# A Flamingo block on one core: TensorE's order at the start of a q unit, and new places for the next block's preparation

## The chip, the cores and the metric

The kernel runs on one NeuronCore of a Trainium2 chip. The metric is the time of one execution on the device, in microseconds (us); the median of several runs is compared. All arithmetic is in 32-bit floating point. A NeuronCore has five engines with queues of their own: TensorE (PE in the profile, with its weight loads listed apart as PEld), VectorE (DVE), ScalarE (ACT), GpSimd (POOL) and SyncE (SP), which here only issues transfers.

## The reference

Eight sequences of 512 tokens with 512 features go through four residual steps, each behind a layer norm: linear attention over 64 context tokens, a feed-forward network of width 2048, a softmax cross attention, and a feed-forward network of eight expert groups with a router. The change lies in the first of them, the linear attention:

```python
x = x + jnp.tanh(g_xattn[0]) * _L0_xattn_ref(_layernorm(x), ctx_2048, Wq, Wg, bg, Wkv, Wo)

# _L0_xattn_ref(query, kv, ...), 16 heads of 32 features
q = query @ Wq.T
gate = sigmoid(query @ Wg.T + bg)
k, v = split(kv @ Wkv.T)
q, k = feature_map(q), feature_map(k)        # x + 1 if x > 0 else exp(x)
kv_summary = einsum('bhsd,bhse->bhde', k, v)
k_sum = k.sum(axis=-2)
z = 1 / (einsum('bhld,bhd->bhl', q, k_sum) + eps)
attn = einsum('bhld,bhde->bhle', q, kv_summary) * z
out = (attn * gate) @ Wo.T
```

## The kernel before, in words

**Blocks and units.** Context keys and values are summed up for all sequences at the start (to about 46 us). Then a loop over eight blocks b, one for each sequence, does the linear attention; after it come eight blocks of each feed-forward network. An attention block has three units: q (`QUp`), gate (`GUp`) and down (`ODown`). Every unit is a product of two matrices that are cut in two by two, done with seven half-sized products instead of eight (the scheme of Strassen and Winograd). Products have the numbers 1 to 7, and a unit runs them in the order 1, 2, 6, 5, 7, 4, 3. I write q1, g4, o7 and so on. Each product is four matmuls of 128x128 by 256 columns, which the profile shows as eight TensorE instructions.

**Banks.** Products 1, 6, 7 and 4 accumulate one onto the other in one PSUM bank (`x`), 5 and 3 in another (`w`), and 2 alone in a third (`z`). Between two products of one bank, ScalarE or VectorE must read the sum so far: in q and gate units ScalarE copies it (line 925), in the down unit VectorE adds it into the residual x (line 1045). There are four banks in rotation for all three units.

**Steps.** `steps` deals out the first five products of a unit, and holds 4 and 3 back as late: they follow the first product of the next unit. So a q unit has seven steps n: q1 (n = 0), then the late o4 and o3 of the down unit before it (n = 1, 2), then q2, q6, q5, q7 (n = 3 to 6). In block 0 there is nothing late, so the steps are q1, q2, q6, q5, q7; in block 1, which has no down unit before it, the late products are g4 and g3 of block 0. Between the q unit and the gate unit stand the numerators (pn) of the block before, and beside the gate unit the denominators (pd). One down unit belongs to the block before: it runs behind the gate unit.

**Order.** A scheduler lays the instructions of each engine in an order of its own, by its own estimates of when each is ready. An engine named in the set `in_order` is exempt: each instruction written while it is in the set is queued behind the one that was written last for that engine. In the attention loop only GpSimd and SyncE are in the set throughout; `with here("vector")` and the like put others in for a few lines. An instruction written outside such lines may still be moved ahead of earlier ones.

**Preparation.** While block b runs, a generator `prep` (`prep_xa0`, which calls `normed`) prepares the input of block b + 1, a piece at each call of `some(prep)`. For blocks 2 to 7 the pieces are:
1. mean and variance of the four token tiles on VectorE (pinned, by `here("vector")`), then 1 / sqrt and shift on GpSimd;
2. normalisation of tiles 0 and 1 on ScalarE, transpose of tile 0 on VectorE (all pinned);
3. normalisation of tiles 2 and 3, transposes of tiles 1 and 2;
4. transpose of tile 3;
5. sixteen transfers issued by SyncE, which bring the pieces to their places in `xnT`, the operand of the next block's products;
6. the generator's last mark, without an instruction.
The rest of the generator (`token_combinations`, the sums `S` of the operand's quarters, lines 689 to 692) is run at step 4 of the down unit. The normalised tiles lie in the same buffer as `spread`, the denominators of the block before; the buffer comes free when `gated` (line 1288) has used these.

**Other work in the loop.** `tick` lets `build_first` prepare the weights of the feed-forward network: transfers, and combinations on VectorE (the tiles `raw_up` and `build_ff_down`), pinned in VectorE's order. `gated` and `attended` (lines 1288 and 1316) join denominators, gate and numerators on VectorE, `features` (lines 675 to 677) is the feature map of q.

Of the kernel before, what the change touches and what calls it, by code (L numbers as in the profile page):

```python
# [31 lines left out]
B, S, D = 8, 512, 512  # L32
# [36 lines left out]
def flamingo_kernel(  # L69
# [26 lines left out]
    @contextmanager  # L96
    def here(*engines):

        new = {*engines} - in_order
        in_order.update(new)  # L100
        yield
        in_order.difference_update(new)
# [59 lines left out]
    def load_x(ph, b):  # L162
        if ph == "xa0" and b % 4 == 3:
            t = awork.tile([P, NT, D], F32, tag="x4", name=f"x_{ph}{b}")
        else:
            t = work.tile([P, NT, D], F32, tag="x", name=f"x_{ph}{b}", bufs=3)
        if ph == "xa0":
            src = x[ts(b, S), :].rearrange("(t p) d -> p t d", p=P)
        else:
            src = between[ph, b]  # L170

        queue = nc.scalar if ph == "xa0" and b > 1 else nc.sync
        with here("scalar"):
            queue.dma_start(out=t, in_=src)
        xs[ph, b] = t
# [3 lines left out]
    def flush():  # L179
        while stores:  # L180
            store_x(*stores.pop(0))
# [767 lines left out]
    def combine_inner(at, prefix=""):  # L949

        a11, a12, a21, a22, s1, s2 = (inner[prefix + k][:, at, :] for k in INNER)
        nc.vector.tensor_tensor(s1, a21, a22, ALU.add)
        nc.vector.tensor_tensor(s2, s1, a11, ALU.subtract)
        nc.vector.tensor_tensor(a21, a11, a21, ALU.subtract)
# [97 lines left out]
    class SplitDown(Unit):  # L1052
# [77 lines left out]
        def gated(self, dst, src):  # L1130
            nc.vector.scalar_tensor_tensor(dst, src, GATE[self.ph], dst, ALU.mult, ALU.add)
# [112 lines left out]
    def denominators(b, q):  # L1244

        pd = psum(f"pd_{b}")
        for c in range(NC):
            nc.tensor.matmul(pd[ts(c, HD), :], lhsT=kv[b][1][:, c, :], rhs=q[:, c, :], start=True, stop=True)
            in_order.add("tensor")
        in_order.discard("tensor")  # L1250
        z = temp(f"z_{b}")
        of_heads = z.rearrange("(n k) t -> n k t", k=8)[:, 0, :]
        over[b] = dram.tile([P // 8, S], F32, tag=f"over{b}", name=f"over_{b}")
        if b == B - 1:
            nc.vector.tensor_scalar(z, pd, ATT_EPS, None, ALU.add)
            yield
            for r in range(2):
                nc.vector.reciprocal(z[:, ts(r, H2)], z[:, ts(r, H2)])
                yield
            nc.sync.dma_start(out=over[b], in_=of_heads)  # L1260
            yield
            return
        nc.scalar.activation(z, pd, AF.Identity, bias=eps, scale=1.0)
        under = dram.tile([P // 8, S], F32, tag=f"under{b}", name=f"under_{b}")
        narrow = small.tile([P, S // 8], F32, tag="narrow", name=f"narrow_{b}")
        with here("gpsimd"):
            nc.gpsimd.dma_start(out=under, in_=of_heads)
            nc.gpsimd.dma_start(out=narrow, in_=under.rearrange("n (u q) -> (n u) q", u=8))
        yield
        yield  # L1270
        nc.vector.reciprocal(narrow, narrow)
        with here("gpsimd"):
            nc.gpsimd.dma_start(out=over[b].rearrange("n (u q) -> (n u) q", u=8), in_=narrow)
        yield
        yield

    def spread(b):

        rows = over[b].rearrange("(c h) t -> c h t", c=NC)
        over[b] = aunits.tile([P, NC, S], F32, tag="over", name=f"spread_{b}")  # L1280
        for h in [slice(0, 2), slice(2, 4)] if b == B - 1 else [slice(0, 4)]:
            for c in range(NC):
                nc.sync.dma_start(out=over[b][ts(c, HD), h], in_=rows[c, h].partition_broadcast(HD))
# [8 lines left out]
    def numerators(b, q):  # L1292

        summary = kv[b][0]
        pn = [psum(f"pn{h}_{b}") for h in range(NC)]
        in_order.add("tensor")
        for c in range(NC):
            for h in range(NC):
                rows = ts(h, HD)
                nc.tensor.matmul(  # L1300
                    pn[h][ts(c, HD), :], lhsT=summary[rows, c, :], rhs=q[rows, c, :], start=True, stop=True
                )
        return pn

    def attended(b, th, pn, ahead=lambda b, th, half: None):

        if b < B - 1:
            a = aunits.tile([P, 2, 2, 2, H2], F32, tag="a", name=f"a_{b}")
        else:
            a = work.tile([P, NC, S], F32, tag="xnT", name=f"a_{b}").rearrange(  # L1310
                "p (r c) (n t) -> p r c n t", c=2, n=2
            )
        for h in range(NC):
            if h % 2 == 0:
                ahead(b, th, h // 2)
            nc.vector.tensor_tensor(
                a[:, :, h // 2, h % 2, :], halves(th[:, h, :]), halves(pn[h]), ALU.mult
            )
        for k in ("s1", "s2"):
            inner["x" + k] = aunits.tile([P, 2, H2], F32, tag=k, name=f"{k}_xa0_{b}")  # L1320
        for r in range(2):
            for c in range(2):
                inner[f"xa{r + 1}{c + 1}"] = a[:, r, c]
# [12 lines left out]
    def steps(units, late=late):  # L1336

        for u in units:
            for n, m in enumerate(u.order[: u.head]):
                yield u, m  # L1340
                if n == 0:
                    yield from late
                    late.clear()
            late.extend((u, k) for k in u.order[u.head :])
# [9 lines left out]
    def some(prep):  # L1354
        if prep not in ready and next(prep, None) == "last":
            ready.add(prep)
# [61 lines left out]
    def tick():  # L1418

        if next(ticks) % 2:  # L1420
            next(builder, None)

    for b in range(B):
        prep = work_list[b + 1][2]
        if b == B // 2 + 1:
            nc.vector.tensor_scalar(b2_sb, b2_sb, gate_ff0, None, ALU.mult)
        q = QUp(b)
        for n, (u, m) in enumerate(steps([q])):
            u.step(m)
            if done and n in (1, 3):  # L1430
                gated(done[0], done[2], n // 2)
            if b == B - 1 and n == 1:
                load_x("ff0", 0)
            if n == 4:
                flush()
            if n in ((4,) if b == 0 else (0, 3, 5) if b < B - 1 else ()):
                some(prep)
            tick()
        if done:
            attended(done[0], done[2], numerators(*done[0:2]))  # L1440
        g = GUp(b)
        den = denominators(b, q.q)
        for n, (u, m) in enumerate(steps([g])):
            u.step(m)
            in_order.discard("tensor")
            if n == 4 and done:
                combine_inner(slice(0, 2), "x")
            tick()
            if n == 1:
                if b + 2 < B:  # L1450
                    load_x("xa0", b + 2)
                elif b + 1 == B:
                    load_x("ff0", 1)
            if b == B - 1 and n > 3:
                next(den, None)
            if n in ((0, 2) if b < B - 1 else (3,)) or n > 2 and not done:
                some(prep)
        if not done:
            for _ in den:
                pass  # L1460
            spread(b)
        if b == B - 1:
            for _ in den:
                pass
            spread(b)
            pn = numerators(b, q.q)
        for n, (u, m) in enumerate(steps([ODown(done[0])] if done else [])):
            u.step(m)
            in_order.discard("tensor")
            if b < B - 1:  # L1470
                next(den, None)
                if n == 6:
                    spread(b)
            elif n == 6:
                attended(b, g.th, pn, gated)
                combine_inner(slice(0, 2), "x")
            if n in ((2,) if b < B - 1 else (6,)):
                some(prep)
            if n == 4 and b < B - 1:
                for _ in prep:  # L1480
                    pass
            tick()
        for _ in prep:
            pass
        done = b, q.q, g.th
# [191 lines left out]
```

## Time and profile before

| what | value |
|---|---|
| median of the runs | 2026.07 us |
| the runs | 2025.39, 2030.78, 2026.07 us |
| the profiled execution, its own time | 2029.55 us |
| its span, first to last instruction | 2027.8 us |
| mean granted TensorE clock | 0.998 |
| TensorE busy with matmuls | 1999.1 us (99%) |
| VectorE, ScalarE, GpSimd busy | 1498.5, 638.7, 226.5 us |
| attention blocks | about 46 to 380 us of the span |

How to read it: all times in the lines of the profile are from the start of the span. In a line of the timeline stand the start, the time taken, the engine, the line of the kernel, the operation, what it writes `<-` what it reads, and how many instructions are merged; in brackets the idle time of the engine just before, and what ended it. `x_xa_down` is bank x of the down unit, `x_q` and `z_q` banks of the q unit, `x_g` of the gate unit; `x_xa` is the residual x. Line L60 is the helper that pins an instruction, so whatever is pinned carries this line. Matmuls are pipelined and their ends are modelled, so lengths of products are read from start to start.

### The profile page before, as it was taken

To read this page: it belongs to the slowest core of one execution; us is meant where nothing else is said; L and a number is where in the kernel's file an instruction comes from. 1 tells how busy PE (TensorE), PEld (TensorE's weight loads), DVE (VectorE), ACT (ScalarE), POOL (GpSimd) and SP (SyncE) were. 2 spreads that over 40 slices of the span, in tenths; PEclk is the share of its full clock that TensorE was granted. 3 is DMA by queue.
4 is the path that set the end of the run, shared out by engine and by line. 5 is a ranking of instruction groups with operands and counts; after the bars stand their busy time and mean duration, and the time that the engine had idled before them with its cause. 6 is when DMAs were issued, how large, how long until landed. Compare 5 with 4: busy or idle time off the path is not lost.

```text
span 2027.8 us, 35126 instructions
## 1 busy us (share of the span) xinstructions
PE 1999.1 (99%) x12332; PEld 1769.2 (87%) x12332; DVE 1498.5 (74%) x3023; ACT 638.7 (31%) x1277; POOL 226.5 (11%) x408
## 2 busy tenths in 40 slices
PE   9999999999999999999999999999999999999998
PEld 5777777799989899999888889898989888898988
DVE  4587788676857677767767687787788686876758
ACT  3533343323241424233334231313232232313122
POOL 3010100201010101011111111110202020110000
PEclk9999999999999999999999999999999999999999
DMA  6366876699999998999987969696978879696875
GB/s 211 125 191 190 243 211 178 219 323 290 319 295 294 303 305 276 301 301 285 294 269 237 315 194 316 205 306 199 289 247 248 280 227 303 194 318 181 279 202 172
DMA packets 319277, 513.72 MB, mean 253 GB/s; under 512 B 44704, under 2 KB 111424, under 8 KB 314112
## 3 DMA queue, kind: packets, MB, share of 16 engines
q1 hardware_dynamic: 303312, 468.28, 73.8%
q0 software_dynamic: 9936, 20.00, 3.5%
q10 hardware_dynamic: 5856, 23.20, 3.2%
q8 instruction: 100, 1.64, 0.3%
q14 instruction: 73, 0.60, 0.1%
HBM read 413.27 MB, written 67.67 MB: 237 GB/s over the span
## 4 chain that ended last, share of the span: by engine, by line
PE 90%; DVE 4%; issue 2%; DMA 2%; ACT 1%; POOL 0%; SPq 0%; DVEq 0%; ACTq 0%; POOLq 0%
PE x_ff L913 27%; PE w_ff L913 13%; PE x_ff_down L1108 13%; PE w_ff_down L1108 9%; PE z_ff L913 7%; PE z_ff_down L1108 4%; PE v_ff_down L1108 4%; PE x_xa_down L1029 2%; PE x_q L913 2%; PE x_g L913 1%; PE w_xa_down L1029 1%; PE pk L60 1%; PE pst L732 1%; PE pr L777 1%; PE pv L60 1%
## 5 line engine op out<-in xcount | busy, mean ns | idle before, releaser
L913 PE MATMUL x_ff<-S_ff,w_ff 128*128 128x256 f32 x1280 | 304.0, 380 | 2.4 <-ACT u_ff L925 2.4
L913 PE MATMUL w_ff<-S_ff,w_ff 128*128 128x256 f32 x1280 | 303.9, 380 | 0.3 <-DVE a_ff L968 0.3
L913 PE MATMUL x_ff<-xnT_ff,w_ff 128*128 128x256 f32 x1280 | 297.4, 380 | 0.0
L925 ACT COPY u_ff<-x_ff 128x512 f32<-128x512 f32 x240 | 139.8, 583 | 446.2 <-PE x_ff L913 411.2
L913 PEld LDWEIGHTS x_ff<-S_ff,w_ff 128*128 128x128 f32 x1280 | 243.7, 191 | 35.8 <-ACT u_ff L925 2.8
L913 PEld LDWEIGHTS w_ff<-S_ff,w_ff 128*128 128x128 f32 x1280 | 241.0, 190 | 36.4 <-issue 2.7
L913 PEld LDWEIGHTS x_ff<-xnT_ff,w_ff 128*128 128x128 f32 x1280 | 239.4, 190 | 33.4 <-issue 2.1
L1108 PE MATMUL x_ff_down<-w_ff_down,split_ff_down 128*128 128x128 f32 x1344 | 162.5, 275 | 1.0 <-DVE split_ff_down L1093 0.9
L1108 PEld LDWEIGHTS x_ff_down<-w_ff_down,split_ff_down 128*128 128x128 f32 x1344 | 156.0, 192 | 1.6 <-DVE split_ff_down L1093 1.1
L913 PE MATMUL z_ff<-xnT_ff,w_ff 128*128 128x256 f32 x640 | 153.1, 380 | 0.0
L913 PEld LDWEIGHTS z_ff<-xnT_ff,w_ff 128*128 128x128 f32 x640 | 119.8, 190 | 20.6 <-issue 5.3
L1122 DVE TENSOR_TENSOR part_ff_down<-part_ff_down 128x128 f32<-128x128 f32 x315 | 83.9, 285 | 71.1 <-ACT part_ff_down L1135 61.9
L497 POOL TENSOR_TENSOR rstd_ff<-var_ff,neg_half 128x4 f32<-128x4 f32 x15 | 15.9, 1061 | 862.1 <-DVE nshift_ff L496 862.1
L1108 PE MATMUL w_ff_down<-w_ff_down,split_ff_down 128*128 128x128 f32 x896 | 107.9, 275 | 0.0
L1108 PEld LDWEIGHTS w_ff_down<-w_ff_down,split_ff_down 128*128 128x128 f32 x896 | 103.9, 192 | 0.0
L973 ACT ACTIVATE a_ff<-a_ff,b_sb 128x256 f32<-128x256 f32 x128 | 58.1, 501 | 92.5 <-DVE a_ff L968 92.5
L1006 DVE TENSOR_TENSOR up_ff<-w_ff,u_ff 128x512 f32<-128x512 f32 x96 | 65.6, 683 | 27.1 <-ACT u_ff L925 27.1
L1108 PE MATMUL x_ff_down<-w_ff_down,a_ff 128*128 128x128 f32 x672 | 83.5, 275 | 1.8 <-ACT a_ff L60 1.8
L968 DVE TENSOR_TENSOR a_ff<-w_ff,u_ff 128x512 f32<-128x512 f32 x64 | 43.9, 685 | 55.3 <-ACT u_ff L925 54.8
L1108 PE MATMUL w_ff_down<-w_ff_down,s_ff 128*128 128x128 f32 x672 | 82.8, 275 | 0.0
L1108 PEld LDWEIGHTS x_ff_down<-w_ff_down,a_ff 128*128 128x128 f32 x672 | 79.7, 192 | 2.6 <-ACT a_ff L60 1.9
L1108 PEld LDWEIGHTS w_ff_down<-w_ff_down,s_ff 128*128 128x128 f32 x672 | 80.0, 192 | 0.8
(271 smaller groups left out, 3375.9 us busy)
## 6 DMA issues: line engine op xcount, KB each, us to landing
w_ff_down<-stream_ff SPq DMA_DIRECT2D x680, 256.0 KB
w_ff<-ff_up SPq DMA_DIRECT2D x560, 256.0 KB
stream_ff<-build_ff_down SPq DMA_DIRECT2D x49, 448.0 KB
x_ff<-x_ff SPq DMA_DIRECT2D x16, 1024.0 KB
share<-shares SPq DMA_DIRECT2D x64, 256.0 KB
ff_up<-build_ff_up SPq DMA_DIRECT2D x42, 256.0 KB
x_ff<-x_xa ACTq DMA_DIRECT2D x8, 1024.0 KB
x_ff<-x_ff ACTq DMA_DIRECT2D x8, 1024.0 KB
```

Source lines behind the costliest of these rows:

```text
L60: made = f(*args, **kw)
L497: nc.gpsimd.tensor_tensor(rstd, var, neg_half, ALU.pow)
L732: nc.tensor.matmul(pst[ts(r, M), :], lhsT=ctxT[:, c, :], rhs=features_of(xnT)[:, c].rearrange("p (u r) q i -> p r u q i", r=2)[:, r], star ...
L777: nc.tensor.matmul(pr[t], lhsT=eT[half, t // 2, :], rhs=c2[half, :], start=True, stop=True)
L913: nc.tensor.matmul(p[:, n, :], lhsT=w[:, c, ts(n, P)], rhs=moving, **self.mark(m, 2 * n + c),)
L925: nc.scalar.copy(self.s[m], p)
L968: nc.vector.tensor_tensor(h, p, s, ALU.add)
L973: nc.scalar.activation(h[:, n, :], p[:, n, :], AF.Gelu, bias=b1_sb[:, f : f + 1])
L1006: nc.vector.tensor_tensor(u, p, s, ALU.add)
L1029: nc.tensor.matmul(p[:, t, :], lhsT=a[:, k, ts(t, P)], rhs=w[k // 2][:, k % 2, :], **self.mark(m, 2 * k + t),)
L1108: nc.tensor.matmul(p[bank][:, place, :], lhsT=operand[k][:, c, :], rhs=w[at // 4][:, ts(at % 4, P)], start=bank not in opened, stop=True, ...
L1122: return lambda: nc.vector.tensor_tensor(m(k), m(k), m(by), ALU.add)
```

## The change

The edit is made in the loop over the attention blocks alone. In the first three steps of every q unit TensorE is put into `in_order`. The calls of `some(prep)` in the q unit move, in blocks 1 to 6, from the steps 0, 3 and 5 to the steps 2, 4 and 5, and the call in the down unit from step 2 to step 1. The calls in the gate unit (steps 0 and 2), those of block 0 and those of the last block stay.

```diff
         q = QUp(b)
         for n, (u, m) in enumerate(steps([q])):
-            u.step(m)
+            with here(*(["tensor"] if n < 3 else [])):
+                u.step(m)
             if done and n in (1, 3):
                 gated(done[0], done[2], n // 2)
             if b == B - 1 and n == 1:
                 load_x("ff0", 0)
             if n == 4:
                 flush()
-            if n in ((4,) if b == 0 else (0, 3, 5) if b < B - 1 else ()):
+            if n in ((4,) if b == 0 else (2, 4, 5) if b < B - 1 else ()):
                 some(prep)
             tick()
...
             elif n == 6:
                 attended(b, g.th, pn, gated)
                 combine_inner(slice(0, 2), "x")
-            if n in ((2,) if b < B - 1 else (6,)):
+            if n in ((1,) if b < B - 1 else (6,)):
                 some(prep)
             if n == 4 and b < B - 1:
                 for _ in prep:
```

## The prediction

> **What bounds the kernel now.** I read the page first, then the windows of the attention blocks, then TensorE's waits, then the timeline around the places where the waits lie. The page's first lines (busy us, share, instructions):
>
> ```profile
> span 2027.8 us, 35126 instructions
> PE 1999.1 (99%) x12332; PEld 1769.2 (87%) x12332; DVE 1498.5 (74%) x3023; ACT 638.7 (31%) x1277; POOL 226.5 (11%) x408
> ```
>
> TensorE is busy for all but 28.7 us of the span, and the change neither adds nor removes a matmul. Only those idle microseconds can be won. The change acts between the first q unit and the last, so I asked for that stretch (length, then busy time of each engine):
>
> ```profile
> 90.00:345.00 255.00, 249.43 (x1300) 199.98 (x1301) 203.51 (x348) 98.16 (x176) 19.06 (x28) 1.00 0.70 208
> ```
>
> Here TensorE idles 5.57 us, at full granted clock (1.00). VectorE is busy 80%, so it has room, but not much. The waits of TensorE from 40 to 400 us say what the idle time is for (total, times, longest):
>
> ```profile
> PE x_xa_down L1029 <- DVE x_xa L1045: 5.8, 8, 0.9
> PE pt_xa L533 <- ACT xn_xa L60: 1.4, 2, 0.9
> PE x_g L913 <- ACT u_g L925: 1.2, 3, 0.7
> PE pd L1248 <- DVE q L677: 1.0, 2, 0.8
> ```
>
> The largest is the down unit's product waiting for VectorE to read its own bank. The timeline at the passage from block 2 to block 3 shows it:
>
> ```profile
> 152.29 1.89 PE L1029 MATMUL x_xa_down<-w_o,a 128*128 128x256 f32 x8
> 154.22 0.75 DVE L1045 SCALAR_TENSOR_TENSOR x_xa<-x_xa_down,gates_half,x_xa 128x512 f32<-128x512 f32 x1 [2.11 <-PE x_xa_down L1029]
> ...
> 155.02 1.13 PE L1029 MATMUL x_xa_down<-w_o,a 128*128 128x256 f32 x4 [0.84 <-DVE x_xa L1045]
> ...
> 155.99 1.89 PE L913 MATMUL x_q<-xnT_xa,w_q 128*128 128x256 f32 x8
> ```
>
> Product 7 of the down unit (o7, 152.29) accumulates in bank x; product 4 (o4, 155.02) goes on in the same bank and must wait until VectorE has read it. The next block's first q product (q1, 155.99) needs another bank and stands behind. The passage into block 5 has the other order, and no wait:
>
> ```profile
> 235.13 1.89 PE L1029 MATMUL x_xa_down<-w_o,a 128*128 128x256 f32 x8
> 235.82 0.69 DVE L689 TENSOR_TENSOR S_xa<-xnT_xa 128x512 f32<-128x512 f32 x1 [0.87 <-DMA xnT_xa<-xn_xa]
> ...
> 236.85 1.89 PE L913 MATMUL x_q<-xnT_xa,w_q 128*128 128x256 f32 x8
> ...
> 237.64 0.74 DVE L1045 SCALAR_TENSOR_TENSOR x_xa<-x_xa_down,gates_half,x_xa 128x512 f32<-128x512 f32 x1
> ...
> 239.44 1.89 PE L1029 MATMUL x_xa_down<-w_o,a 128*128 128x256 f32 x8
> ```
>
> **The change, part by part.** *TensorE's order.* From block 1 on, the first three steps of a q unit are q1, then the down unit's late products o4 and o3. Pinned, they run in that order. Blocks 5, 6 and 7 already have q1 ahead of o4, so nothing is won there. Blocks 2, 3 and 4 have it behind. Unstalled, a product's eight instructions take 1.73 us from start to start (150.56 to 152.29). From o7 to o4 it is 2.93 (111.71 to 114.64), 2.73 (152.29 to 155.02) and 2.74 (193.64 to 196.38). So the three stalls cost 1.20 + 1.00 + 1.01 = 3.21 us. With q1 between, o4 comes 1.73 us after o7's end, and VectorE needs about 1.0 (154.02 to 155.02): covered with 0.7 to spare. If that cover is gone because VectorE is late, the 1.0 comes back in that block.
>
> The pin adds a wait: q1 may now meet an xnT that has not landed, with o4 and o3 queued behind it. SyncE issues the sixteen xnT transfers in about 10 us:
>
> ```profile
> 101.24 10.73 SPq L60 DMA_DIRECT2D xnT_xa<-xn_xa  x16
> ```
>
> In block 5 they are issued until 234.29 (223.75 + 10.54) and VectorE's wait for them ends at 235.82, so landing is 1.53 after the last issue. By that estimate they land at 113.5, 153.0 and 195.2 in blocks 2 to 4, and o7 ends at 113.44, 154.02 and 195.37. Only block 2 is on the edge: I take 0.15 us of new wait, bounds 0 and 0.6. [...]
>
> Block 1 has no down unit before it; its late products are g4 and g3 of the gate unit. There the scheduler put half of q1 at 69.11, while g7 waited for ScalarE's copy of bank x (68.93 to 69.52). The pin forbids this: q1 goes behind g7, and the hole of about 0.5 us stays open. Cost 0.45, bounds 0 and 0.9 (the half's four instructions take 0.86). In block 0 the three steps are q1, q2, q6, which run in that order today: nothing.
>
> *Preparation.* By the diff the calls in the q unit move from steps 0, 3, 5 to 2, 4, 5: later by two and by one, the third unmoved. The call in the down unit moves from step 2 to 1; it only reaches the generator's last mark and issues no instruction. The change was announced as beginning the preparation three steps sooner; the diff does not do that: the statistics begin two steps later, after o3. The first call issues 4 x (0.66 + 0.17) + 2 x 0.16 = 3.6 us on VectorE and two operations on GpSimd (1.0 to 1.9 and 0.2 to 0.65), the second two normalisations on ScalarE (0.80 each) and one transpose on VectorE (0.69). None issues a DMA, and between the old and new places nothing is queued on SP or POOL that they pass; on VectorE they pass the reads of o4 and o3, on ScalarE the copy and exponentials of q6. With o7 ending at 154.02 in block 3, q1, o4 and o3 end 5.2 later and the read 0.9 after that: statistics start near 160.0 instead of 155.67, 4.4 us later. Who waits? The normalisations, and these wait for something else (block 2, GpSimd and then ScalarE):
>
> ```profile
> 124.72 0.19 POOL L60 TENSOR_TENSOR nshift_xa<-nshift_xa,rstd_xa 128x4 f32<-128x4 f32 x1
> ```
> ```profile
> 136.63 2.93 ACT L60 ACTIVATE xn_xa<-x_xa,nshift_xa,rstd_xa 128x512 f32<-128x512 f32 x4 [1.82 <-DVE th L1288]
> ```
>
> The scale is ready at 124.91, but the normalisation begins at 136.63, when VectorE's gating (L1288) has freed the buffer it writes. The slack in blocks 1 to 6 is 9.4, 11.7, 12.6, 10.0, 19.0 and 6.7 us. All exceed 4.4. Block 5's statistics, which today float up to 225.23, move furthest: to after o3's read (243.10 + 0.75), so 3.6 us of VectorE and at most 2.6 of GpSimd later the scale is ready near 250.1, still ahead of 255.59, where the normalisation begins. So I cost the move at nothing, bounds -0.5 (VectorE freer right after o7) and +1.0 (one read behind a 0.66 statistic).
>
> Sum: -3.21 + 0.15 + 0.45 = -2.6 us. The profiled execution took 2029.55 (span 2027.8 and 1.75 around it), 3.5 above the median 2026.07; the sum is a difference, so I take it from the median: 2023.5.
>
> **The rivals.** *Slower: the transfer becomes the bound.* If the 4.4 us of later statistics go through normalisation, transpose and the 10 us of issues, q1 finds xnT late, and nothing stands in for it. With the landing ahead of o7's end by -0.1, 1.0, 0.2, 1.0, 3.5 and 4.7 us in blocks 2 to 7, the full delay would cost 4.5 + 3.4 + 4.2 + 3.4 + 0.9 = 16.4, less 2.6: 2039.9. A delay of d costs 4d - 2.1; it eats the gain at 1.2 us per block and passes +0.3% at 2.7. For it: VectorE's 80%, on a chain that goes through it three times. Against it: the slacks above, and block 6, whose statistics already run at 280.33 to 286.7, after which xnT lands 4.7 us early. [...]
>
> *No change.* VectorE reads o7's bank late (behind the token combinations, as at 237.64) and the wait for it moves to o4 behind q1: the 3.2 us are not won, 2026.
>
> *Faster.* The gate unit's and denominators' waits vanish too. All idle time from 90 to 345 us is 5.57, which gives 2020.5; to pass -0.3% the feed-forward blocks, whose order is computed anew, must lose one of theirs (the longest is 2.4 us): 2018 to 2019.
>
> **How the numbers follow.** 0.3% is 6.1 us, about what a measurement of this kernel can tell from no change. The forecast has 0.50; its own range, with costs at their bounds and the 2.7 us by which runs of before differ from their middle, is 2020 to 2028. No change has 0.16, the slower rival beyond +0.3% (or a reshuffled feed-forward order of that size) 0.20, the faster one beyond -0.3% 0.14. Same is 0.50 + 0.16 = 0.66. The range reaches to 2018.5, part of the faster case, and to 2034, a delay of 3.2 us per block; beyond them I leave about 0.2.
>
> **What would show it.** Right: TensorE's wait of the down unit for L1045 falls from 5.8 to about 3 us, and q1 stands before all of o4 in blocks 2 to 4. The statistics start after o3's read, and ScalarE's normalisation still waits for L1288. Wrong: q1 waits for the xnT transfers, or normalisation waits for GpSimd; or TensorE's idle time from 90 to 345 stays at 5.6; or the difference lies after 400 us.

## The result, and the profile after

The changed kernel takes 2030.7 us (median of 14 runs, 2028.1 to 2036.1), the kernel before 2025.6 in the same runs. The ratio is 1.0027, with a 95% interval of 1.0019 to 1.0035: slower by about 5.5 us, where I had forecast 2.6 less. The profiled execution took 2035.35 us. It lies 4.7 above its median, that of before 4.0 above its own.

The page and the attention stretch of the changed kernel (length; then busy time of TensorE, weight loads, VectorE, ScalarE, GpSimd; granted clock, DMA share, GB/s):

```profile
span 2033.3 us, 35119 instructions
PE 2003.3 (99%) x12332; PEld 1770.6 (87%) x12332; DVE 1500.6 (74%) x3023; ACT 639.5 (31%) x1277; POOL 225.5 (11%) x408
90.00:345.00 255.00, 246.40 (x1268) 196.32 (x1266) 199.71 (x335) 95.82 (x172) 17.46 (x28) 0.99 0.66 200
```

TensorE's idle time there rose from 5.57 to 8.60 us, and the granted clock fell from 1.00 to 0.99. TensorE's waits from 40 to 400 us say which waits came and went (total, times, longest):

```profile
PE x_xa_down L1029 <- DVE x_xa L1045: 4.5, 6, 0.9
PE x_xa_down L1029 <- DVE qs_q L1214: 3.3, 4, 1.2
PE pd L1248 <- DVE q L677: 2.6, 2, 1.8
PE x_g L913 <- ACT u_g L925: 1.4, 3, 0.7
```

The wait the change aims at fell from 5.8 to 4.5. The second line is new at this size (0.3 us in blocks 1 to 6 before): o1 waits for VectorE to read q3 (`qs_q`), because o1 needs q3's bank. The third grew from 1.0.

The passage from block 2 to block 3 is now as the change wants it. o7, q1 and o4 follow at 1.72 and 1.73 us without a wait, and VectorE's read of o7's bank lies beside q1:

```profile
151.37 1.89 PE L1029 MATMUL x_xa_down<-w_o,a 128*128 128x256 f32 x8
153.09 1.89 PE L60 MATMUL x_q<-xnT_xa,w_q 128*128 128x256 f32 x8
153.29 0.75 DVE L1045 SCALAR_TENSOR_TENSOR x_xa<-x_xa_down,gates_half,x_xa 128x512 f32<-128x512 f32 x1 [2.10 <-PE x_xa_down L1029]
...
154.82 1.89 PE L60 MATMUL x_xa_down<-w_o,a 128*128 128x256 f32 x8
```

To find where the time went I divided every block in two on TensorE's timeline: the gate stage, from the first numerator matmul (pn) to the start of o7, and the passage, from there to the next pn. I call this table the ledger (blocks 1 to 6, in us, one execution of each kernel):

| kernel | gate stage, blocks 1 to 6 | sum | passages, sum | both |
|---|---|---|---|---|
| before | 26.30, 25.39, 26.33, 26.47, 26.85, 25.28 | 156.62 | 86.93 | 243.55 |
| after | 26.76, 27.28, 31.31, 27.07, 27.69, 26.58 | 166.69 | 84.11 | 250.80 |

The passages won 2.82 us. The gate stages, for which my sum had no term, lost 10.07. Outside these blocks the profiles differ by 2.06 in the start (block 0's first product began between 43.8 and 46.5 us in all the profiles, whatever the kernel) and by less than 0.4 in all the rest.

The gate stage of block 2 on VectorE, before and then after, shows the loss. L1214 is the read of q3, L1288 the gating:

```profile
133.46 0.69 DVE L1214 TENSOR_TENSOR qs_q<-w_q,u_q 128x512 f32<-128x512 f32 x1 [2.09 <-PE w_q L913]
134.06 2.48 DVE L1288 SCALAR_TENSOR_TENSOR th<-th,spread 128x512 f32<-128x512 f32 x4
```
```profile
128.48 2.49 DVE L1288 SCALAR_TENSOR_TENSOR th<-th,spread 128x512 f32<-128x512 f32 x4
130.89 2.47 DVE L1316 TENSOR_TENSOR a<-th,pn 128x512 f32<-128x512 f32 x4
...
137.29 0.65 DVE L1214 TENSOR_TENSOR qs_q<-w_q,u_q 128x512 f32<-128x512 f32 x1
```

Before, VectorE reads q3 at once and gates afterwards. After, four gating operations, four of `attended`, the transposes and other work stand ahead of the read, which comes 6.8 us after TensorE has gone on from q3. TensorE feels it in block 2 at o1, the first product of the down unit, whose bank is that of q3:

```profile
135.73 0.62 PE L60 MATMUL pd<-q,ksum 128*32 128x512 f32 x1
...
138.00 1.56 PE L1029 MATMUL x_xa_down<-w_o,a 128*128 128x256 f32 x6 [1.22 <-DVE qs_q L1214]
...
141.65 1.05 PE L60 MATMUL pd<-q,ksum 128*32 128x512 f32 x4
```

This shows a second cost too: the denominators (pd) are cut in two, since the last q features come late as well, and each part takes TensorE about 1 us.

How late the read of q3 starts after TensorE's next product, in blocks 1 to 6 (us; 0.2 is at once):

| kernel | 1 | 2 | 3 | 4 | 5 | 6 |
|---|---|---|---|---|---|---|
| before | 0.2 | 0.2 | 0.2 | 6.0 | 6.0 | 4.8 |
| after | 0.2 | 6.8 | 7.0 | 6.6 | 6.1 | 5.4 |
| pin alone | 0.2 | 5.3 | 6.8 | 6.0 | 4.6 | 5.0 |
| preparation alone | 0.2 | 0.2 | 0.2 | 0.2 | 6.0 | 4.0 |

### The profile page after: what moved, and what is told of

Its sections match the earlier page's. It is cut to its first block, busy times and chain, and to the rows that moved or that the text cites. A ratio compares the mean times of both kernels' runs of the same rounds, so it can differ in the third digit from the quotient of the medians.

```text
span 2033.3 us, 35119 instructions
## 1 busy us (share of the span) xinstructions
PE 2003.3 (99%) x12332; PEld 1770.6 (87%) x12332; DVE 1500.6 (74%) x3023; ACT 639.5 (31%) x1277; POOL 225.5 (11%) x408
## 4 chain that ended last, share of the span: by engine, by line
PE 88%; DVE 5%; DMA 2%; SPq 2%; ACT 1%; issue 1%; POOL 0%; DVEq 0%; ACTq 0%; POOLq 0%
PE x_ff L913 27%; PE w_ff L913 13%; PE x_ff_down L1108 13%; PE w_ff_down L1108 9%; PE z_ff L913 7%; PE z_ff_down L1108 4%; PE v_ff_down L1108 4%; SPq L60 2%; PE x_xa_down L1029 2%; PE x_q L913 1%; PE x_g L913 1%; PE pst L732 1%; PE pr L777 1%; PE pv L60 1%; DVE a L1316 1%
```

## The experiments

**Theory A**, made from the two traces: the pin moves the q unit on TensorE, the scheduler then lays VectorE's gating ahead of the read of q3 in blocks 2 and 3 too, and the late read and the cut denominators cost more than the passages bring. **Rival B** ("theory B" in what was expected): the moved preparation does it. **Rival C**: VectorE's chain of gating, transposes and xnT transfers sets the end, so whatever is won in the gate stage returns as q1 waiting for xnT. **Rival D**, later: an early read of q3 is simply a better order, with or without the change. Where experiments 3, 5, 7 and 8 say "the whole change", the down unit's call of `some(prep)` stays at its old step 2; it only reaches the generator's last mark, which issues no instruction.

**1 and 2. Each half alone.** The first has only the pin, the second only the moved calls in the q unit:

```diff
-            u.step(m)
+            with here(*(["tensor"] if n < 3 else [])):
+                u.step(m)
```
```diff
-            if n in ((4,) if b == 0 else (0, 3, 5) if b < B - 1 else ()):
+            if n in ((4,) if b == 0 else (2, 4, 5) if b < B - 1 else ()):
```

> TensorE's program order in the first three steps of a q unit, with the preparation's calls at their old steps 0, 3, 5. Theory A (the pin makes the scheduler lay VectorE's gating block, 4 gatings, 4 attended products, 4 transposes and builder sums, ahead of its read of q3 and of the last q features, and the gate stage then waits): as slow as the whole change, 4 to 7 us above before; TensorE's waits for qs_q and q (VectorE) from 90 to 345 us sum to 4 to 7 us, against 1.5 before, and the wait of o4 for o7's read is gone in blocks 2 to 4. Theory B (the later statistics crowd VectorE): 2 to 3 us faster than before, those waits near 1.5 us.

> The preparation's calls at steps 2, 4, 5, without the pin. Theory A: within 2 us of before; VectorE reads q3 before gating in blocks 2 and 3, TensorE's waits for qs_q and q stay at 1.5 us or less, and the three or more stalls of about 1 us where o4 follows o7 stay. Theory B: 4 to 7 us slower than before, waits for qs_q and q at 4 to 7 us.

The pin alone: 2030.9 us, ratio 1.0021 (1.0012 to 1.0030). Passages 85.58, gate stages 162.37, so 5.75 more there than before; the time is what theory A wanted, but the waits for qs_q and q come to 1.4 + 1.5 us, fewer than its 4 to 7. The other idle time of its gate stages is waits for ScalarE's copy of a gate bank (2.2) and for other VectorE work (1.3). The preparation alone: 2029.7, ratio 1.0017 (1.0009 to 1.0026). Neither theory had that: it is slower by more than A's 2 us, without B's waits. Its waits for qs_q did not grow; it lost 2.76 in the gate stages (denominators cut in five blocks instead of three) and 1.44 in the passages, where o4 now stood ahead of q1 in four:

```profile
PE x_xa_down L1029 <- DVE x_xa L1045: 7.5, 10, 0.9
```

So each half does harm, by an order that the scheduler lays anew (read from the traces; no run isolates it for the preparation), and they overlap: the pin costs 0.21%, the preparation 0.17%, both together 0.27%.

**3 and 4. Reads and features of q4 and q3 first**, on the changed kernel and on the one before:

```diff
-            if m == 4:
-                self.rest(self.part(2, 1, p, None))
-            if m == 3:
-                self.rest(self.part(1, 2, p, self.s[6]))
+            if m in (4, 3):
+                first = tc.high_priority() if self.tag.startswith("q") else ExitStack()
+                with first:
...
```

> The whole change, and in addition the reads of q4 and q3 (with their feature maps) get the scheduler's first priority, so VectorE reads q3 in the middle of the gating block instead of behind it. Theory A: the waits of the gate stage for qs_q and q go, 1.5 us or less; the gain at the passages stays: 2 to 5 us faster than before, 7 to 10 faster than the whole change. Theory B: still 3 us or more slower than before, since the statistics are as late as in the change.

> The kernel before with only the reads of q4 and q3 at first priority. Theory A: in blocks 4 to 6, where before too gates first, the waits for qs_q and q (1.5 us in all) go; passages unchanged: 0 to 2 us faster than before. Theory B says nothing of it beyond that; were it to gain as much as the whole change with the reads first does, the pin would be worth nothing.

Both missed: 2035.2 us, ratio 1.0036 (1.0023 to 1.0049), and 2030.9, ratio 1.0022 (1.0013 to 1.0030). In the changed kernel the gate stages did shrink, to 156.71; in the kernel before they stayed, at 156.17. But the last block (from the seventh pn to the feed-forward) got 4.05 us longer in both, where TensorE waits longer for VectorE. The passages of the kernel before got 3.35 longer, since o4 now stood ahead of q1 into blocks 5 and 6 as well, and in the changed kernel q1 waited for transfers:

```profile
PE x_q L60 <- DMA xnT_xa<-xn_xa: 4.0, 2, 2.7
```

In the changed kernel this is rival C, and the mechanism of the slower rival in my prediction: it exists, but behind the first limit. The edit was too broad. The next ones move one instruction, and the denominators.

**5 and 6. Denominators in one go**, on the changed kernel and on the one before. The groups that need the last features come first, so that all four groups run when these are there:

```diff
-        for c in range(NC):
+        for c in (2, 3, 0, 1):
             nc.tensor.matmul(pd[ts(c, HD), :], lhsT=kv[b][1][:, c, :], rhs=q[:, c, :], start=True, stop=True)
```

> The whole change, and beside it one loop turned round: the denominators of a block start with the two groups that need the last q features, so that all four groups of matmuls run in one go and not in two halves. Theory A (the loss of 10.1 us in the gate stages of blocks 1 to 6 is VectorE's late read of q3 plus the denominators' product being cut in two, about 1.0 us for each cut in blocks 1 to 5): the cuts go, TensorE waits once and longer for the q features instead; 2 to 5 us less than the whole change, 2025.5 to 2028.5. Rival C (the stage is set by VectorE's chain gating, transposes, transfers of xnT: any gain comes back as q1 waiting for xnT): within 1.5 us of the whole change, and the trace shows waits of q1 for xnT of 1.5 us or more.

> The kernel before with the loop over the denominators turned round as in the other run, nothing else. Theory A: before has cuts in blocks 1, 4 and 5, about 1.0 us each; 1 to 3 us less than before (2022.5 to 2024.5). Rival C: within 1 us of before.

2031.0 us, ratio 1.0024 (1.0015 to 1.0033): no better than the change. 2027.2, ratio 1.0007 (0.9998 to 1.0016): no better than before. Theory A missed both. The cuts did go in every block, yet the late read stayed and o1 waited longer for it (in the first kernel):

```profile
PE x_xa_down L1029 <- DVE qs_q L1214: 5.9, 4, 2.2
PE x_g L913 <- ACT u_g L925: 2.7, 3, 1.9
PE x_q L60 <- DMA xnT_xa<-xn_xa: 1.3, 1, 1.3
```

So theory A's two costs are not a sum: while the read is late, removing the cut only lengthens the wait for it. Rival C had the time of the first kernel right, and the third line is its sign, a little under the 1.5 us that it asked for. But its mechanism took back only 1.1 us in the passages (84.11 to 85.23); most of the loss stayed in the gate stages (163.43).

**7 and 8. One read first.** Only VectorE's read of q3 has priority, its features stay where they were; in the second kernel the denominators are in one go as well:

```diff
-                nc.vector.tensor_tensor(t, p, s, ALU.add)
+                with tc.high_priority() if (r, c) == (1, 2) and self.b < B - 1 else ExitStack():
+                    nc.vector.tensor_tensor(t, p, s, ALU.add)
```

> The whole change, with one instruction for each block given first priority: VectorE's read of the third q product (the one that frees the bank in which o1 of the next unit accumulates). The q features keep their late place, unlike in the run that moved reads and features together. Theory A: TensorE's wait for this read (0.34 us before, 3.3 after) falls under 0.5, the waits for q features stay near 1.8; 2 to 5 us less than the whole change (2025.5 to 2028.5). Rival C: gating and transposes move back by the 0.7 us of the read at most, so q1 waits for xnT and the time stays within 1.5 us of the whole change.

> Both edits on top of the whole change: the read of the third q product first, and the denominators in one go. Theory A: the gains add, 5 to 9 us less than the whole change, that is 0 to 4 less than before (2021.5 to 2025.5). Rival C: q1 waits for xnT; no better than the better of the two single edits.

2025.4 us, ratio 0.9994 (0.9985 to 1.0003): the whole loss is gone. With both edits 2023.0, ratio 0.9984 (0.9975 to 0.9993), less than either kernel. Theory A had expected both, the first a little less good. VectorE in block 2 with the read first (the second edit not made) shows how little had to move. The read (L1215 there, the gating L1289) has slipped in between the third and the fourth gating operation:

```profile
128.29 1.89 DVE L1289 SCALAR_TENSOR_TENSOR th<-th,spread 128x512 f32<-128x512 f32 x3
130.46 0.69 DVE L1215 TENSOR_TENSOR qs_q<-w_q,u_q 128x512 f32<-128x512 f32 x1 [0.28 <-PE w_q L913]
131.07 0.68 DVE L1289 SCALAR_TENSOR_TENSOR th<-th,spread 128x512 f32<-128x512 f32 x1
```

Not only the read moved with this edit: the denominators of blocks 2 and 3 are no longer cut (those of 1, 4 and 5 still are), and the idle time of the gate stages fell from 8.5 to 3.9 us. The wait for qs_q is no longer among TensorE's waits from 40 to 400 us of either kernel. Gate stages and passages: 158.82 and 84.09, with both edits 152.83 and 85.79. Rival C falls for the single edit (no wait for xnT at all). With both it holds in one place, into block 2, where q1 waits 1.4 us for xnT. The same pair of kernels gives the price of one cut, since in block 5 neither waits for anything: 25.98 with the denominators cut, 24.82 without, so about 1.17 us. (The pin alone gives the same 25.98 for a cut in block 2 without a wait.)

**9 to 12. Is it the change or the mends?** Read first alone on the kernel before, then both mends (read first, denominators in one go) with nothing, the pin, or the preparation; experiment 8 is the fourth of this square.

> The kernel before with first priority for VectorE's read of the third q product, nothing else. Theory A (the change loses its time because its pin lets the scheduler put this read behind the gating): in the kernel before the read is late only in blocks 4 to 6 and costs TensorE 0.3 us, so this edit is worth 0 to 1 us here, against 5.3 when it stands on the changed kernel: 2025 to 2026.5. Rival D (the read's priority is simply a better order, whatever the change): 3 us or more less than before, 2023 or under.

> The kernel before with both mends (read of the third q product first, denominators in one go) and without the change. By its order o4 stands ahead of q1 in the passages into blocks 2 to 6. Theory A: the passage stalls stay, 1.0 us each in three to five passages, and block 1 keeps its hole filled (0.5 won); so 2.5 to 4.5 us more than the changed kernel with both mends (2023.0): 2025.5 to 2027.5. Rival D (the mends do it all, the change is worth nothing): 2022 to 2024.

> Only the pin of the change, with both mends. Theory A (the moved preparation costs and brings nothing once the read is early): as the changed kernel with both mends, 2023.0 within 1 us. Rival E (statistics two steps later make xnT late; the changed kernel with both mends waits 1.4 us for xnT in one block): 1 to 2 us less, 2021 to 2022.

> Only the moved preparation, with both mends and no pin. Theory A: o4 still stands ahead of q1, in the passages into blocks 2 to 6, about 1.0 us each: 2.5 to 5 us more than the changed kernel with both mends: 2025.5 to 2028. Rival D: 2022 to 2024.

| | without mends: ratio to before | with both mends: median, ratio to before |
|---|---|---|
| nothing | 1 | 2029.6 us, 1.0013 (1.0004 to 1.0022) |
| pin | 1.0021 (1.0012 to 1.0030) | 2023.1 us, 0.9982 (0.9973 to 0.9991) |
| preparation | 1.0017 (1.0009 to 1.0026) | 2027.9 us, 1.0006 (0.9997 to 1.0015) |
| both (the change) | 1.0027 (1.0019 to 1.0035) | 2023.0 us, 0.9984 (0.9975 to 0.9993) |

The read first on the kernel before, without the pin, gives 2028.3, ratio 1.0006 (0.9997 to 1.0015). I had expected 2025 to 2026.5: it won 2.66 us in the gate stages and gave back 2.87 in the passages (o4 now ahead of q1 in blocks 5 and 6 as well) and 1.62 in the last block. Both mends without the change missed too: I expected 2025.5 to 2027.5 and it is 2029.6, since the last block is 4.06 longer there as well, by TensorE's waits for VectorE. The other two came as theory A said. Rival D falls twice: neither the read first nor both mends make the kernel before faster. With the mends the pin is worth 6.5 us (2029.6 to 2023.1), without them it costs 0.21%; against the kernel before, pin and mends together win 0.18%. TensorE's waits from 40 to 400 us, both mends without the pin and then with it:

```profile
PE x_xa_down L1029 <- DVE x_xa L1045: 7.9, 9, 1.1
```
```profile
PE x_xa_down L1029 <- DVE x_xa L1045: 4.5, 5, 1.5
```

Of the 6.5, the passages give 3.7 (89.40 to 85.69) and the last block 2.5 (55.59 to 53.13 from its pn to the feed-forward); why the pin shortens the last block no run here shows. The moved preparation is worth nothing beside the pin (0.9984 and 0.9982), and the 1.3 us wait for xnT into block 2 is there with the old preparation too, so rival E of experiment 11 falls.

## Why the prediction was wrong, point by point

**The passages: right.** I forecast 1.20, 1.00 and 1.01 us won into blocks 2, 3 and 4; the ledger has 1.18, 1.00 and 0.67. The third is short for the reason that I had given (the cover is gone when VectorE is late): there o7 itself waited 0.88, and VectorE put four token combinations ahead of the read of its bank.

**xnT into block 2: no wait in the changed kernel,** where I took 0.15:

```profile
99.14 10.71 SPq L60 DMA_DIRECT2D xnT_xa<-xn_xa  x16
...
110.08 1.99 PE L1029 MATMUL x_xa_down<-w_o,a 128*128 128x256 f32 x8 [0.60 <-DVE x_xa L1045]
111.91 1.89 PE L60 MATMUL x_q<-xnT_xa,w_q 128*128 128x256 f32 x8
```

The issues end at 109.85, so by the prediction's 1.53 the transfers land near 111.4, ahead of q1. This is luck: o7 itself began 0.60 late, behind VectorE. (The 0.11 by which the passage exceeds the unstalled 13.90 stands in front of q1, which starts 1.83 us after o7 instead of 1.73; q1 starts 1.83 after o7 into block 4 as well, where o7 had also waited and xnT was long there.) With the pin alone o7 is not late, its last issue ends at 110.52, and q1 stands idle for 0.69; with the pin and the denominators in one go it waits 1.3 to 1.4. My upper bound of 0.6 was an estimate for which no run shows a source.

**Block 1: right in size, but not the end of it.** The pin alone lengthens the stretch from block 0's first product to block 1's pn by 0.55 (I took 0.45). The moved preparation, which I had at 0, shortens the same stretch by 0.58, so the whole change has -0.03.

**The preparation: right on its chain, wrong in its price.** Statistics of the next block start in block 3 at 159.3 (forecast 160.0), the scale is ready before the normalisation in every block, and three of the normalisations still end their idle time on L1288 (0.22, 2.27 and 2.87 us). I found nobody whom the move delays by data. "I cost the move at nothing" was wrong all the same: alone it cost 0.17%, and its trace shows other orders on VectorE and TensorE (experiment 2).

**The step that failed: the sum ended at the passages.** I wrote that "Blocks 5, 6 and 7 already have q1 ahead of o4, so nothing is won there" and gave the gate stages no term, as if an instruction that the diff does not name kept its place. My only mention of an order computed anew was for the feed-forward blocks, which moved by 0.4 us at most. The missing term is 10.07 us. From the traces: TensorE's waits in the gate stages rose by 5.8 (2.7 to 8.5; 4.6 of it are waits for the read of q3 and for features of q), two more cuts at 1.17 make 2.3, one stretch at half clock 1.7; 0.3 is not assigned. Experiment 7 shows the cause, with 9 as its control: an early place for one instruction per block takes the changed kernel from 1.0027 to 0.9994 of before (5.3 us between the medians), and does nothing for the kernel before (1.0006).

The trace of before held a warning, if not a clear one. In its blocks 2 and 3, entered with o4 ahead of q1, the read of q3 was prompt; in blocks 5 and 6, entered with q1 ahead, it was 6.0 and 4.8 us late, and block 5's gate stage 1.5 longer than block 2's (block 6's was not longer). Block 4 breaks the pattern: it has o4 ahead, and the read is late all the same; so does block 5 of the preparation alone. In both the late read comes first, and the passage behind it then has q1 ahead. Experiment 9 shows that the tie works this way too: with the read prompt in blocks 4 and 5, the passages behind them went back to o4 first. None of the seven kernels without the pin has a block from 1 to 5 with both the prompt read and q1 ahead behind it. Pinned order and early read together give both, and this fits that neither wins alone. That pin and late read hang together through the scheduler's estimates is argued from the orders; the estimates are in no trace.

**The slower rival** had the right sign and the wrong mechanism: no wait of q1 for xnT shows in the changed kernel. Its full size was wrong as well (2039.9 against 2030.7). The sign I named for it, normalisation waiting for GpSimd, did not appear. **No change** had VectorE's late read of o7's bank: seen into block 4 alone, worth 0.3.

## What to carry to other kernels

When part of a schedule is pinned and the rest is laid by estimates, price every stage behind the pin, not just the one that the pin mends: look in the trace of before for blocks that already have the pinned order, and compare their other stages with the rest. A bank's reader is the instruction to look at first; one read per block, 5 to 7 us late in five blocks, cost more here than three stalls of 1 us. A pin that loses time can still be right: with two mends beside it, it is worth 6.5 us against the same kernel without the pin, and 0.18% against the kernel before.

## What the runs showed of the hardware

**Stretches at half clock.** Apart from the kernel's start and end, the granted TensorE clock fell to 0.5 for 3.413 us at a time: twice in the changed kernel (from 180.95 and from 1075.24 us) and once in the kernel before (from 1069.21). In the other profiles, sums over 4 us show about 1.7 us of clock lost each time. Over all fourteen profiles I found 20 such drops, in thirteen of them; experiment 4 showed none. The starts in one profile lie whole multiples of 3.4133 us apart: 262 between the two of the changed kernel, 311 between 1069.21 and the drop at the start (7.66) in the kernel before, 36 between two of experiment 5 (180.98 and 303.86). I divided each profile into windows of that length, laid by its drops. Those around the drop in block 3 of the changed kernel:

```profile
174.14:177.55 3.41, 2.95 (x14) 2.26 (x12) 3.41 (x7) 1.06 (x2) 0.00 (x0) 1.00 0.55 211
177.55:180.96 3.41, 1.41 (x4) 0.48 (x5) 3.38 (x7) 1.52 (x3) 0.00 (x0) 1.00 0.22 55
180.96:184.37 3.41, 3.41 (x10) 2.70 (x9) 2.17 (x4) 1.18 (x4) 0.00 (x0) 0.50 0.39 99
```

TensorE was busy for 1.41 of 3.41 us (it waited for the features, then for ScalarE), and the next window ran at half clock, which makes the product in it 3.27 us long instead of 1.73:

```profile
178.86 1.04 PE L1248 MATMUL pd<-q,ksum 128*32 128x512 f32 x2 [1.77 <-DVE q L677]
180.59 3.47 PE L913 MATMUL x_g<-S_xa,w_g 128*128 128x256 f32 x8 [0.69 <-ACT u_g L925]
183.86 2.15 PE L1029 MATMUL x_xa_down<-w_o,a 128*128 128x256 f32 x8
```

I read these windows from 50 to 1997 us in the two kernels, and in the twelve experiments from about 53 to 361 and from 668 to 972 us. Ten of them had TensorE busy for 1.65 us or less (0.93 to 1.65). Nine of the ten were followed by a window at half clock, and no window with 1.80 or more was. The tenth, at 218.09 us in experiment 8, had 1.49 busy and a full clock (1.00) after it; why stays open. So about 1.8 us of idle time inside one window mostly cost another 1.7 here (half of 3.41). In these rows the idle time of one window told more than the length of a wait: in the changed kernel with denominators in one go, a wait of 2.20 us in block 2 left its two windows busy for 2.67 and 1.96 us and brought no drop, while in block 3 a wait of 2.00 and one of 0.44 left a window busy for 1.49, and the next ran at half clock.

**Cut denominators.** The four groups of 32-column matmuls took TensorE about 1.06 us together (259.41 to 260.47 in block 5 of experiment 8), and each half of them about 1.05 us alone in block 2 of the changed kernel (135.72 to 136.77, and the 1.05 from 141.65 in the lines above); the cut cost 1.17 in the ledger.
